# Mamba-2 stage of a four-layer network: VectorE in program order, convolution steps deferred, the group norm applied after the output product

## Chip, cores and metric

The kernel runs on one core of a Trainium2 chip. The metric is the device time of one execution in microseconds (us), as the median of three runs. A profile is one further execution under the hardware profiler.

## The reference

Four layers act on x of shape 2 x 1024 x 256 (float32), each as x = x + attention(LN x), then x = x + ffn(LN x):

- layer 0: causal attention with 16 heads and rotary positions; SwiGLU
- layer 1: grouped attention (16 query heads, 4 key heads) with two gates; SwiGLU
- layer 2: a Mamba-2 block in the place of attention; a ternary-weight feed-forward
- layer 3: a simple attention of rank 32; a mixture of 16 experts, the two best per token

The Mamba-2 block, to which the change belongs, computes (cut from the reference; H = 32 heads of 64, G = 8 groups, state S = 32):

```python
zxbcdt = (hidden_states @ W_in + b_in) * mup_vector
z, xBC, dt = ...                      # 2048, 2048 + 2*256, 32 columns
xBC = silu(causal_conv4(xBC) + conv_b)
x, B, C = ...                         # 2048, 256, 256 columns
dt = softplus(dt + dt_bias);  a = exp(dt * -exp(A_log))
state[t] = a[t] * state[t-1] + dt[t] * x[t] (outer) B[t]
y = state . C + D_param * x
y = y * silu(z)
y = y * rsqrt(mean over each group's 256 channels of y*y + eps) * norm_w
return y @ W_out + b_out
```

Since the group norm scales each token and group by one number, it may be applied before the product with W_out, or to the product's eight parts, one for each group, behind it.

## The kernel before

**Layout.** x stays in SBUF as 16 token tiles of 128 x 256, `xs[i]`. Before each stage `norm` (L93) writes the normalised x and its transpose `xnT`. One function, `tile_blocks_kernel`, holds all stages one after the other, and names its engines at its start (L46): V is VectorE, S ScalarE, G GpSimd (POOL in the profile), PE TensorE. Its helpers `norm`, `add_to_x` (L128), `evacuate` (L140, a copy from PSUM that ScalarE and VectorE take in turn), `softmax` (L150) and `ffn` (L157) use these names. Where nothing else is said, a scheduler decides each engine's order; `tc.keep_in_program_order(...)` fixes an instruction's place, in the order of the program, among those of its engine that are so marked, and `tc.high_priority()` asks for an early place.

**Mamba stage.** The 2048 tokens are 8 blocks of 256 (4 per batch). All TensorE and ScalarE work of the stage is kept in program order (helpers `pe`, `pe_t`, `act`, whose lines L702, L705 and L708 show in the profile); VectorE and POOL are scheduled. A block's x, B and C live channel by token: `quads[blk, q]` for q = 0 to 3 (groups q and q + 4, 128 x 4 x 256) and `bcs[blk]`. Per block:

- `steps2`: dt and dA from the product `dp`, a chain of small VectorE instructions (first `u`, L743).
- `project(blk, f)`, ten per block: product `xp_ps` in a PSUM bank of tag A (two banks, also for `gate` and the norm's `rg`); ScalarE writes xp and the fourth tap's part; six VectorE instructions (L809) add the other three taps of the convolution. `silu` follows.
- `prepare(blk, t, hs)`, four per block (two halves of 128 tokens, two pairs of quads): per group, POOL makes `dm` (L834), PE `lp`, ScalarE the decay `ml`. `from_start` makes `cd` from `rp`; `to_end` makes `de` from `ep` and `bt` (L886) from `bp`; `times_dt` transposes x (`xtp`) and VectorE makes `xd` (L850); `masked` makes `cp`, and VectorE `cm` (L897) and, shared with POOL, the masked `ml` (L900).
- `scan(blk, t, hs)`: `yp` gets xd times ml and the old state times cd. Then, for each quad, POOL makes dx = D x (L968, a tile with one buffer), and VectorE adds it to `yp` (L971). `sp` feeds the new state.
- `gate(blk, f)`, eight per block, one block behind: product `zp`; ScalarE's Silu, POOL's product with y (L1003), ScalarE's Square, in series. `squares` sums the squares of each group on PE into the bank Q (`qp`).
- The norm: `scales` takes the root (ScalarE) and the reciprocal of a 128 x 256 tile (L1020). `scaled(blk, q)` spreads the eight rows over the partitions by PE with the constant selT (`rg`, two products of 128 x 256 per quad) and VectorE multiplies y (L1028, 128 x 1024).
- `output(blk, t)`: 16 products `op` into one PSUM bank of tag Q, and `add_to_x` (L129).

The order is written out by hand. For each block four quarters i = 0 to 3 go by; in each, `prepare` works for the next quarter's scan, calls `scan` through `now()`, and at four places calls `fill()`, which takes a share of a list `work`: gates and squares of the block before (i = 0, 1), the projections of the next block (2, 2, 3, 3 in the four quarters), the norm (i = 2) and the output product (i = 3). What is left of the list comes at the quarter's end.

**Behind the Mamba stage** come the ternary feed-forward (`ffn`) and layer 3. There, routing finds the place of each token's two copies, and 32 indirect transfers (L1269) scatter the normalised tokens to `sent` in 47 slots of 128 rows. `attention(0)`, batch 0's attention, stands behind the scatter in the program. The expert loop then does for each slot s: load weights and rows, transpose the rows (`xgp`), VectorE copy `xgT` (L1332), 16 products `hp`, Silu `eh` (L1338), products `eo`, VectorE copy `ey` (L1343), store to `done` by POOL's queue. `attention(1)` follows, with a mask add, maximum, exponential, transposes, products and an add to x for each of eight query tiles; and at the end, for each of the 16 tiles of x, two indirect gathers `back` (L1351, eight buffers) that VectorE adds to x (L1356), and the store.

The code below has the lines of the profile.

Of the kernel before, what the change touches and what calls it, by code (L numbers as in the profile page):

```python
# [23 lines left out]
ALU = mybir.AluOpType  # L24
# [19 lines left out]
def kernel(ctx: ExitStack, tc: tile.TileContext, a: dict, out: bass.AP):  # L44
# [623 lines left out]
    selT = kept("selT", [P, 8, P])  # L668
    load(selT, a["selT"])
# [11 lines left out]
    with work_pool("l2") as pool, tc.tile_pool(  # L681
# [27 lines left out]

        def small(tag, blk, shape=(P, 2, 32), bufs=1):  # L710
            return pool.tile(list(shape), F32, tag=tag, name=f"{tag}_{blk}", bufs=bufs)
# [18 lines left out]
        def steps2(blk):  # L730
# [11 lines left out]
            with tc.high_priority():  # L742
                V.tensor_tensor(u, dp, heads(0), ALU.add)  # L743
# [29 lines left out]
        def project(blk, f):  # L773
# [32 lines left out]
            for n in range(2):  # L806
                for k in range(3):
                    c = 4 * (f + n) + k
                    V.scalar_tensor_tensor(  # L809
                        dst[:, n], xp[:, n, k : k + 256], cw[:, c : c + 1], dst[:, n],  # L810
                        op0=ALU.mult, op1=ALU.add,
                    )

        def silu(t_):
            tf = t_.rearrange("p f t -> p (f t)")
            act(tf, tf, AF.Silu)
# [4 lines left out]
        def prepare(blk, t, hs, fill, now):  # L821
# [22 lines left out]
            def times_dt(q):  # L844
# [4 lines left out]
                with tc.high_priority():  # L849
                    V.tensor_tensor(  # L850
                        xd.rearrange("p (a j) c -> p a j c", a=2),
                        tp.rearrange("p (a f) (h c) -> p a (f h) c", a=2, h=2),
                        by_quad(dt[:, t, :], q).unsqueeze(3).to_broadcast([P, 2, 4, 64]), ALU.mult,
                    )
# [20 lines left out]
            def to_end():  # L875
# [9 lines left out]
                with tc.high_priority():  # L885
                    V.tensor_copy(bt, bp)  # L886
                c["de"], c["bt"] = de, bt

            def masked(q):
# [6 lines left out]
                with tc.high_priority():  # L896
                    V.tensor_tensor(cm, cp, le.unsqueeze(1).to_broadcast([P, 2, P]), ALU.mult)  # L897
# [27 lines left out]
        def scan(blk, t, hs):  # L925
# [39 lines left out]
            for n, q in enumerate(qs):  # L965
                y = quads[blk, q][:, :, ct].rearrange("p (a f) t -> p a f t", a=2)
                dx = pool.tile([P, 2, 2, P], F32, tag="dx", name=f"dx{nm}_{q}", bufs=1)
                G.tensor_tensor(  # L968
                    dx, y, by_quad(Dp, q).unsqueeze(3).to_broadcast([P, 2, 2, P]), ALU.mult
                )  # L970
                V.tensor_tensor(y, yps[n], dx, ALU.add)  # L971
# [19 lines left out]
        def gate(blk, f):  # L991
# [31 lines left out]
        def scaled(blk, q):  # L1023
            rp = bank("A", [P, 2, 256], f"rg{blk}_{q}")
            for a in range(2):
                pe(rp[:, a], selT[:, q + 4 * a, :], gates[blk], True, True)
            y = quads[blk, q].rearrange("p (a f) t -> p a f t", a=2)
            V.tensor_tensor(y, y, rp.unsqueeze(2).to_broadcast([P, 2, 2, 256]), ALU.mult)  # L1028
# [20 lines left out]
        for blk in range(N2 + 1):  # L1049
            for i in range(4):  # L1050
# [424 lines left out]
```

## Time and profile before

| | |
|---|---|
| median of three runs | 3618.98 us (3617.89 to 3619.17) |
| the profiled execution | 3631.11 us, its span 3629.4 us |
| granted TensorE clock, mean | 0.930 |
| busy: PE, DVE, ACT, POOL | 3170.7, 1798.1, 1182.3, 1072.7 us |

By stretches of the program (the table of stretches; us):

| stretch | length | PE busy | DVE busy | clock |
|---|---|---|---|---|
| layer 0 (0 to 760) | 760 | 689.3 | 405.2 | 0.96 |
| layer 1 (to 2013) | 1253 | 1146.9 | 634.5 | 0.96 |
| Mamba (to 3072) | 1059 | 882.9 | 596.1 | 0.89 |
| ternary feed-forward (to 3215) | 143 | 135.1 | 38.7 | 0.98 |
| norm, routing, scatter, attention(0) (to 3362) | 147 | 76.5 | 52.1 | 0.68 |
| expert loop (to 3557) | 195 | 187.2 | 37.4 | 0.99 |
| attention(1), gather, store (to 3629.4) | 72 | 52.9 | 34.0 | 0.83 |

How the profile is read: DVE is VectorE, ACT ScalarE, PEld TensorE's weight loads, SP the queue that issues most DMAs. A group line gives the source line, the engine, the operation, what it writes and reads (names without numbers), shapes and count; then busy time and the mean duration in ns; then the engine's idle time just before such instructions and who ended it. A granted clock under 1 says that TensorE was throttled in part of the stretch. The line of an instruction that goes through a helper is the helper's.

### The profile page before, as it was taken

Reading aid. Unit: us, or ns where it says so; the run is one execution under the profiler, and the core shown is the slowest. Engines: PE = TensorE matmul, PEld = TensorE weight load, DVE = VectorE, ACT = ScalarE, POOL = GpSimd, SP = SyncE. Lnnn points to the kernel's source line nnn. Section 1 sums busy time; section 2 is a strip of 40 time slices with the busy share of each in tenths; the row PEclk is TensorE's granted clock in tenths of the full one; section 3 lists DMA queues with packets and bytes.
Section 4 is the critical chain, followed back from the end, with each engine's and each line's share of the span. In section 5 each row is a group of like instructions: output and inputs, shape, how many; then the busy total and the mean of one; then the engine's idle time right before and its main releaser. Section 6 shows DMA issues by size and latency. Waiting matters only on the chain.

```text
span 3629.4 us, 43224 instructions
## 1 busy us (share of the span) xinstructions
PE 3170.7 (87%) x16608; PEld 2062.8 (57%) x16608; DVE 1798.1 (50%) x3500; ACT 1182.3 (33%) x2089; POOL 1072.7 (30%) x1215
## 2 busy tenths in 40 slices
PE   7999999898998998988999788888788788984997
PEld 5666665544544544544555556666566566552885
DVE  5666553255465455565413775556546643241124
ACT  1133333332322322322312554644644542111111
POOL 2011101032233232232200565554555551013113
PEclk9999999799999999999999888989899899977998
DMA  4000100300000000000001000000000000003892
GB/s 135 7 19 13 48 1 1 127 1 1 1 0 1 1 1 0 1 12 30 1 21 35 1 1 1 1 1 1 1 1 1 1 17 14 1 4 110 287 319 79
DMA packets 80733, 117.24 MB, mean 32 GB/s; under 512 B 7664, under 2 KB 60848, under 8 KB 78992
## 3 DMA queue, kind: packets, MB, share of 16 engines
q1 hardware_dynamic: 66864, 91.67, 7.7%
q0 software_dynamic: 5328, 14.56, 1.2%
q10 hardware_dynamic: 8336, 8.26, 0.7%
q8 instruction: 131, 2.15, 0.2%
q14 instruction: 74, 0.61, 0.1%
HBM read 91.65 MB, written 22.81 MB: 32 GB/s over the span
## 4 chain that ended last, share of the span: by engine, by line
PE 61%; DVE 19%; ACT 8%; POOL 5%; issue 5%; DMA 1%; ACTq 0%; POOLq 0%; DVEq 0%; another core or an unknown queue 0%
PE op L126 7%; PE sc L126 6%; PE m L245 5%; DVE xx L809 4%; PE sc L245 4%; PE tp L631 3%; PE op L702 3%; PE d L126 3%; PE g L126 3%; PE u L126 3%; PE eo L126 2%; PE hp L126 2%; PE mx L245 2%; PE lp L702 2%; PE acc L245 2%
## 5 line engine op out<-in xcount | busy, mean ns | idle before, releaser
L622 POOL TENSOR_SCALAR pr<-pr,r,gate 128x128 f32<-128x128 f32 (+7 forms) x256 | 211.0, 826 | 535.6 <-DVE r L621 473.7
L154 ACT ACTIVATE pr<-sc,nmax 128x128 f32<-128x128 f32 (+7 forms) x272 | 201.3, 741 | 477.1 <-DVE nmax L153 411.3
L126 PE MATMUL sc<-kT,qT 128*128 128x512 f32 (+3 forms) x768 | 316.5, 515 | 41.9 <-POOL qT L578 29.0
L126 PE MATMUL op<-pT,v 128*128 128x512 f32 x576 | 287.0, 617 | 19.9 <-DVE pT L146 13.2
L809 DVE SCALAR_TENSOR_TENSOR xx<-xp,w2r,xx 128x256 f32<-128x256 f32 x384 | 223.5, 634 | 44.0 <-ACT xx L708 40.6
L339 ACT ACTIVATE pT<-sc 128x1024 f32<-128x1024 f32 (+1 forms) x160 | 150.3, 939 | 270.8 <-PE sc L245 270.8
L631 PEld LDWEIGHTS tp<-cst,pr 128*128 128x128 f32 x1152 | 137.7, 142 | 131.6 <-POOL pr L622 69.1
L153 DVE TENSOR_REDUCE nmax<-sc 128x1 f32<-128x128 f32 (+7 forms) x272 | 203.1, 754 | 6.2
L631 PE MATMUL tp<-cst,pr 128*128 128x128 f32 x1152 | 183.1, 282 | 17.6 <-POOL pr L622 13.4
L126 PEld LDWEIGHTS sc<-kT,qT 128*128 128x128 f32 x768 | 134.6, 206 | 112.4 <-POOL qT L578 39.3
L126 PEld LDWEIGHTS op<-pT,v 128*128 128x128 f32 x576 | 105.0, 192 | 153.5 <-issue 62.7
L144 ACT COPY pT<-tp 128x512 f32<-128x512 f32 (+2 forms) x160 | 91.9, 575 | 295.2 <-PE tp L631 255.2
L245 PE MATMUL sc<-qk,qk 32*128 32x256 f32 (+1 forms) x1280 | 169.2, 382 | 8.9 <-ACT pT L339 8.3
L146 DVE COPY pT<-tp 128x512 f32<-128x512 f32 (+2 forms) x152 | 103.6, 682 | 142.1 <-PE tp L631 134.7
L702 PE MATMUL lp<-dm,cst 128*128 128x512 f32 x256 | 149.2, 705 | 22.5 <-DVE u L743 11.4
L342 POOL TENSOR_SCALAR_AFFINE_SELECT pT<-pT 128x512 f32<-128x512 f32 x64 | 40.8, 637 | 428.2 <-ACT pT L339 424.8
L834 POOL TENSOR_TENSOR dm<-cst,dA 128x512 f32<-128x512 f32 x128 | 142.9, 1124 | 64.5 <-PE lp L702 62.6
L245 PE MATMUL mx<-qk,qk 32*128 32x256 f32 (+1 forms) x1280 | 144.7, 387 | 10.8 <-DVE nm L314 3.0
L245 PEld LDWEIGHTS sc<-qk,qk 32*128 32x128 f32 x1280 | 105.0, 186 | 66.6 <-issue 31.2
L708 ACT ACT_TABLE_LOAD x110 | 141.1, 1283 | 2.0
L151 DVE TENSOR_TENSOR sc<-sc,cst 128x128 f32<-128x128 f32 x272 | 79.6, 296 | 125.4 <-PE sc L126 120.5
L702 PE MATMUL xp_ps<-xnT,w2x 128*128 128x256 f32 x512 | 132.1, 404 | 7.1 <-ACT xx L708 6.7
(294 smaller groups left out, 6322.8 us busy)
## 6 DMA issues: line engine op xcount, KB each, us to landing
we<-in_L_W SPq DMA_DIRECT2D x94, 512.0 KB, 5.5
sent<-none ACTq DMA_DIRECT2D x1, 6016.0 KB
xg<-sent SPq DMA_DIRECT2D x47, 128.0 KB, 5.4
done<-ey POOLq DMA_DIRECT2D x47, 128.0 KB
gu<-in_L_gu SPq DMA_DIRECT2D x4, 1024.0 KB
x<-in_x ACTq DMA_DIRECT2D x16, 128.0 KB, 5.3
dn<-in_L_dn SPq DMA_DIRECT2D x2, 1024.0 KB, 8.3
tabs<-in_L_rope SPq DMA_DIRECT2D x2, 1024.0 KB
```

Source lines behind the costliest of these rows:

```text
L126: PE.matmul(out_, lhsT=lhsT, rhs=rhs, start=first, stop=last)
L146: V.tensor_copy(dst, src)
L153: V.tensor_reduce(nmax, sc[:, :n], axis=AX.X, op=ALU.max, negate=True)
L154: S.activation(pr, sc[:, :n], AF.Exp, bias=nmax, accum_out=total)
L245: tc.keep_in_program_order(PE.matmul(out_, lhsT=lhsT, rhs=rhs, start=first, stop=last))
L339: S.activation(pT[:, :, :, :w], sc[:, :, :, :w], AF.Exp, scale=0.25)
L622: G.tensor_scalar(pr[:, :n], pr[:, :n], r, gate[:, i, 4 * g + j : 4 * g + j + 1], op0=ALU.mult, op1=ALU.mult,)
L631: PE.transpose(tp[:, j, :], prs[j][:, kb * P : (kb + 1) * P], ident)
L702: tc.keep_in_program_order(PE.matmul(out_, lhsT=lhsT, rhs=rhs, start=first, stop=last))
L708: tc.keep_in_program_order(S.activation(*args, **kw))
L809: V.scalar_tensor_tensor(dst[:, n], xp[:, n, k : k + 256], cw[:, c : c + 1], dst[:, n], op0=ALU.mult, op1=ALU.add,)
L834: G.tensor_tensor(dm, le.unsqueeze(1).to_broadcast([P, 4, P]), dAc[:, 4 * g : 4 * g + 4].unsqueeze(2).to_broadcast([P, 4, P]), ALU.mult,)
```

## The change

The change touches six things:

1. An object `Ordered` stands for VectorE and marks each of its instructions to be kept in program order; V is set to it. The two `tc.high_priority()` blocks around `xd` and `cm`, and those around `u` and `bt`, go.
2. The six convolution instructions of a `project` are put on a list and issued by `convolve()`, which the next `fill()`, the next `silu` or the end of a quarter calls.
3. D x is no longer made by POOL: 32 VectorE instructions per block (128 x 128) compute y times D plus `yp` from PSUM.
4. The norm is applied behind the output product: the eight rows of sums are copied (`qs`), transposed by PE to tokens by groups (`qt`), root and reciprocal work on 128 x 16; `output` makes one product per group, in banks of tag A, and VectorE adds each, times its token's scale, to x. `scaled`, selT and its load go.
5. The Square of a gate is issued behind the next gate.
6. The work list: outputs of the first token half fall in quarter 2 and of the second in quarter 3, gates and projections alternate, and the silus move (quads 2 and 3 into the next block's first quarter).

The diff, without the four places where only a `tc.high_priority()` goes and without the constant selT on the host:

```diff
@@ before L665, after L665 @@
     nwD = rest2[:, 428 : 460]
     nw, Dp = nwD[:, 0:16], nwD[:, 16:32]
-    selT = kept("selT", [P, 8, P])
-    load(selT, a["selT"])
 
@@ before L707, after L705 @@
         def act(*args, **kw):
             tc.keep_in_program_order(S.activation(*args, **kw))
 
+        class Ordered:
+
+
+            def __getattr__(self, op):
+                return lambda *args, **kw: tc.keep_in_program_order(getattr(nc.vector, op)(*args, **kw))
+
+        V = Ordered()
+        convs = []
+
+        def convolve():
+            while convs:
+                convs.pop(0)()
+
         def small(tag, blk, shape=(P, 2, 32), bufs=1):
             return pool.tile(list(shape), F32, tag=tag, name=f"{tag}_{blk}", bufs=bufs)
 
@@ before L803, after L813 @@
                     bias=tap3[:, 1, g : g + 1], scale=tap3[:, 0, g : g + 1],
                 )
             G.tensor_copy(hist[:, f : f + 2, :], xp[:, :, 256:259])
-            for n in range(2):
-                for k in range(3):
-                    c = 4 * (f + n) + k
-                    V.scalar_tensor_tensor(
-                        dst[:, n], xp[:, n, k : k + 256], cw[:, c : c + 1], dst[:, n],
-                        op0=ALU.mult, op1=ALU.add,
-                    )
+
+            def step(n, k):
+                c = 4 * (f + n) + k
+                V.scalar_tensor_tensor(
+                    dst[:, n], xp[:, n, k : k + 256], cw[:, c : c + 1], dst[:, n],
+                    op0=ALU.mult, op1=ALU.add,
+                )
+
+            convs.extend(lambda n=n, k=k: step(n, k) for n in range(2) for k in range(3))
 
         def silu(t_):
+            convolve()
             tf = t_.rearrange("p f t -> p (f t)")
             act(tf, tf, AF.Silu)
 
@@ before L963, after L973 @@
                                     a == 1 and jj >= 2,
                                 )
             for n, q in enumerate(qs):
-                y = quads[blk, q][:, :, ct].rearrange("p (a f) t -> p a f t", a=2)
-                dx = pool.tile([P, 2, 2, P], F32, tag="dx", name=f"dx{nm}_{q}", bufs=1)
-                G.tensor_tensor(
-                    dx, y, by_quad(Dp, q).unsqueeze(3).to_broadcast([P, 2, 2, P]), ALU.mult
-                )
-                V.tensor_tensor(y, yps[n], dx, ALU.add)
+                for a in range(2):
+                    for f in range(2):
+                        y, g = quads[blk, q][:, 2 * a + f, ct], 2 * q + 8 * a + f
+                        V.scalar_tensor_tensor(
+                            y, y, Dp[:, g : g + 1], yps[n][:, a, f], op0=ALU.mult, op1=ALU.add
+                        )
             if not last:
                 if hs == 0:
                     c["sp"] = bank("T", [P, 2, 256], f"sp{nm}", bufs=1)
@@ before L1001, after L1011 @@
                 g = f + n
                 act(zs[:, n], zp[:, n], AF.Silu, bias=bm[:, g : g + 1], scale=mup_f[:, g : g + 1])
             G.tensor_tensor(y, y, zs, ALU.mult)
+            gates[blk, f] = zs, y
+
+        def square(blk, f):
+            zs, y = gates[blk, f]
             act(zs, y, AF.Square)
-            gates[blk, f] = zs
 
         def squares(blk, f, n_th):
             if n_th == 0:
@@ before L1010, after L1023 @@
             g = f // 2
             for n in range(2):
                 pe(
-                    gates[blk], sel[:, 7 - g : 7 - g + P], gates[blk, f][:, n],
+                    gates[blk], sel[:, 7 - g : 7 - g + P], gates[blk, f][0][:, n],
                     n_th == 0 and n == 0, n_th == 7 and n == 1,
                 )
 
+        def sums(blk):
+
+            qs = pool.tile([8, 256], F32, tag="qs", name=f"qs_{blk}", bufs=1)
+            V.tensor_copy(qs, gates[blk][0:8, :])
+            gates[blk] = qs
+
         def scales(blk):
-            rs = pool.tile([P, 256], F32, tag="rs2", name=f"rs2_{blk}", bufs=1)
-            act(rs, gates[blk], AF.Sqrt, scale=1.0 / 256.0, bias=eps_t)
+            qt = bank("Q", [P, 2, 8], f"qt{blk}", bufs=1)
+            for t in range(2):
+                tc.keep_in_program_order(
+                    PE.transpose(qt[:, t, :], gates[blk][:, t * P : (t + 1) * P], ident[0:8, 0:8])
+                )
+            rs = pool.tile([P, 2, 8], F32, tag="rs2", name=f"rs2_{blk}")
+            act(rs, qt, AF.Sqrt, scale=1.0 / 256.0, bias=eps_t)
             V.reciprocal(rs, rs)
             gates[blk] = rs
 
-        def scaled(blk, q):
-            rp = bank("A", [P, 2, 256], f"rg{blk}_{q}")
-            for a in range(2):
-                pe(rp[:, a], selT[:, q + 4 * a, :], gates[blk], True, True)
-            y = quads[blk, q].rearrange("p (a f) t -> p a f t", a=2)
-            V.tensor_tensor(y, y, rp.unsqueeze(2).to_broadcast([P, 2, 2, 256]), ALU.mult)
-
-        def output(blk, t):
-            op = bank("Q", [P, D], f"op2_{blk}_{t}", bufs=1)
+        def output(blk, t, gs):
+
+            op = bank("A", [P, 2, D], f"op2_{blk}_{t}_{gs[0]}")
             ct = slice(t * P, (t + 1) * P)
-            fs = [f for q in range(4) for f in (2 * q, 2 * q + 1, 2 * q + 8, 2 * q + 9)]
-            for n, f in enumerate(fs):
-                pe(op, quads[blk, n // 4][:, n % 4, ct], w2o[f // 8][:, f % 8, :], n == 0, n == 15)
-            add_to_x(2 * blk + t, op)
+            for n, g in enumerate(gs):
+                for f in range(2):
+                    pe(
+                        op[:, n], quads[blk, g % 4][:, 2 * (g // 4) + f, ct],
+                        w2o[g // 4][:, 2 * g % 8 + f, :], f == 0, f == 1,
+                    )
+            for n, g in enumerate(gs):
+                x = xs[2 * blk + t]
+                V.scalar_tensor_tensor(
+                    x, op[:, n], gates[blk][:, t, g : g + 1], x, op0=ALU.mult, op1=ALU.add
+                )
 
         V.memset(hist, 0.0)
         V.memset(state, 0.0)
@@ before L1051, after L1076 @@
                 t, hs = i // 2, i % 2
                 work = []
                 nxt, prv = blk + 1, blk - 1
-                if prv >= 0:
-                    if i < 2:
-                        four = xorder[4 * i : 4 * i + 4]
-                        for n, f in enumerate(four):
-                            work.append(lambda f=f: gate(prv, f))
-                            at_ = 4 * i + n
-                            if at_ >= 2:
-                                work.append(lambda n=at_ - 2: squares(prv, xorder[n], n))
-                        if i == 1:
-                            gated = [lambda n=n: squares(prv, xorder[n], n) for n in (6, 7)]
-                            gated.append(lambda: scales(prv))
+                old = prv >= 0
+
+                def outputs(t):
+                    return [lambda t=t, q=q: output(prv, t, (q, q + 4)) for q in range(4)]
+
+                if i == 0 and 0 < blk < N2:
+                    work += [lambda: silu(quads[blk, 2]), lambda: silu(quads[blk, 3])]
+                new = []
                 if nxt < N2:
                     pairs = ([16, 18], xorder[0:2], xorder[2:5], xorder[5:8])[i]
-                    for f in pairs:
-                        work.append(lambda f=f: project(nxt, f))
-                        if i == 3 and prv >= 0 and f != pairs[2]:
-                            work.append(lambda t=(f != pairs[0]): output(prv, int(t)))
+                    new = [lambda f=f: project(nxt, f) for f in pairs]
+                other = []
+                if old and i < 2:
+                    for n in range(4 * i, 4 * i + 4):
+                        def gated(n=n):
+                            gate(prv, xorder[n])
+                            if n:
+                                square(prv, xorder[n - 1])
+
+                        other.append(gated)
+                        if n >= 2:
+                            other.append(lambda n=n: squares(prv, xorder[n - 2], n - 2))
+                if old and i == 2:
+                    other.append(lambda: (squares(prv, xorder[6], 6), square(prv, xorder[7])))
+                    other.append(lambda: (squares(prv, xorder[7], 7), sums(prv)))
+                    other.append(lambda: scales(prv))
+                    other += outputs(0)
+                if old and i == 3:
+                    other += outputs(1)
+                while new or other:
+                    if new:
+                        work.append(new.pop(0))
+                    for _ in range(-(-len(other) // (len(new) + 1))):
+                        work.append(other.pop(0))
+                if nxt < N2:
                     if i == 1:
-                        work.append(lambda: (steps2(nxt), silu(bcs[nxt])))
-                    if i == 1 and prv >= 0:
-                        work[-2:-2] = gated
+                        work.append(lambda: (silu(bcs[nxt]), steps2(nxt)))
                     if i == 2:
                         work.append(lambda: silu(quads[nxt, 0]))
-                        work.append(lambda: silu(quads[nxt, 1]))
                     if i == 3:
-                        work.append(lambda: silu(quads[nxt, 2]))
-                        work.append(lambda: silu(quads[nxt, 3]))
-                elif i == 1 and prv >= 0:
-                    work += gated
-                if prv >= 0:
-                    if i == 2:
-                        for q in range(4):
-                            work.append(lambda q=q: scaled(prv, q))
-                    if i == 3 and nxt >= N2:
-                        work.append(lambda: output(prv, 0))
-                        work.append(lambda: output(prv, 1))
+                        work.insert(1, lambda: silu(quads[nxt, 1]))
                 if blk < N2:
                     if i < 3:
                         after = (blk, (i + 1) // 2, (i + 1) % 2)
@@ before L1095, after L1125 @@
                     share = len(work) // 5 or 1
 
                     def fill():
+                        convolve()
                         for _ in range(share):
                             if work:
                                 work.pop(0)()
@@ before L1109, after L1140 @@
                     else:
                         fill()
                         now()
+                convolve()
                 for w in work:
                     w()
     tc.no_sync_barrier()
```

In the changed kernel's built order TensorE has 9235 instructions (9283 before), VectorE 3782 (3502), ScalarE 1830 (1836), POOL 1156 (1220) and SP 515 (516). Up to the Mamba stage the instructions are the same, but for the load of selT.

More of the change, by code (lines that the diff above doesn't have):

```diff
@@ L741, in steps2 @@
             u = small("u", blk)
-            with tc.high_priority():
-                V.tensor_tensor(u, dp, heads(0), ALU.add)
+            V.tensor_tensor(u, dp, heads(0), ALU.add)
             V.tensor_tensor(u, u, heads(1), ALU.mult)
@@ L848, in times_dt @@
                 xd = pool.tile([P, 8, 64], F32, tag="xd", name=f"xd{nm}_{q}", bufs=3)
[L849 to L853, printed above, removed]
-                    )
+                V.tensor_tensor(
+                    xd.rearrange("p (a j) c -> p a j c", a=2),
+                    tp.rearrange("p (a f) (h c) -> p a (f h) c", a=2, h=2),
+                    by_quad(dt[:, t, :], q).unsqueeze(3).to_broadcast([P, 2, 4, 64]), ALU.mult,
+                )
                 c["xd"][q] = xd
@@ L884, in to_end @@
                 bt = pool.tile([P, 2, P], F32, tag="bt", name=f"bt{nm}")
-                with tc.high_priority():
-                    V.tensor_copy(bt, bp)
+                V.tensor_copy(bt, bp)
                 c["de"], c["bt"] = de, bt
@@ L895, in masked @@
                 cm = pool.tile([P, 2, P], F32, tag="cm", name=f"cm{nm}_{q}")
-                with tc.high_priority():
-                    V.tensor_tensor(cm, cp, le.unsqueeze(1).to_broadcast([P, 2, P]), ALU.mult)
+                V.tensor_tensor(cm, cp, le.unsqueeze(1).to_broadcast([P, 2, P]), ALU.mult)
                 for a in range(2):
@@ L965, in scan @@
             for n, q in enumerate(qs):
-                y = quads[blk, q][:, :, ct].rearrange("p (a f) t -> p a f t", a=2)
-                dx = pool.tile([P, 2, 2, P], F32, tag="dx", name=f"dx{nm}_{q}", bufs=1)
-                G.tensor_tensor(
-                    dx, y, by_quad(Dp, q).unsqueeze(3).to_broadcast([P, 2, 2, P]), ALU.mult
-                )
-                V.tensor_tensor(y, yps[n], dx, ALU.add)
+                for a in range(2):
[4 more added lines that the diff above has]
+                        )
             if not last:
@@ L1030, in output @@
-        def output(blk, t):
-            op = bank("Q", [P, D], f"op2_{blk}_{t}", bufs=1)
-            ct = slice(t * P, (t + 1) * P)
-            fs = [f for q in range(4) for f in (2 * q, 2 * q + 1, 2 * q + 8, 2 * q + 9)]
-            for n, f in enumerate(fs):
-                pe(op, quads[blk, n // 4][:, n % 4, ct], w2o[f // 8][:, f % 8, :], n == 0, n == 15)
-            add_to_x(2 * blk + t, op)
+        def output(blk, t, gs):
+            op = bank("A", [P, 2, D], f"op2_{blk}_{t}_{gs[0]}")
+            ct = slice(t * P, (t + 1) * P)
+            for n, g in enumerate(gs):
[8 more added lines that the diff above has]
+                    x, op[:, n], gates[blk][:, t, g : g + 1], x, op0=ALU.mult, op1=ALU.add
+                )
@@ L1374, in _constants @@
     cst[:, C_SEL + 7] = 1.0
-    selT = np.zeros((P, 8, P), f)
-    selT[np.arange(8), np.arange(8), :] = 1.0
     pos = np.arange(T, dtype=f)
@@ L1394, in _constants @@
     steps = np.concatenate([np.arange(16) * 128, np.arange(NSLOT)]).astype(f)
-    return {"cst": cst, "selT": selT, "L0_rope": rope0, "L1_rope": rope1, "eidx": eidx, "steps": steps}
+    return {"cst": cst, "L0_rope": rope0, "L1_rope": rope1, "eidx": eidx, "steps": steps}
 def _laid_out(i):
```

## The prediction

> **What bounds the kernel now.** I read the table of stretches first, one window for each of the five steady Mamba blocks (from one block's first output product `yp` to the next one's). One of them, and the sum (columns: length; busy time of PE, PEld, DVE, ACT, POOL; granted clock; DMA):
>
> ```profile
> 2406.67:2536.40 129.73, 109.20 (x669) 81.97 (x668) 75.92 (x130) 68.51 (x108) 64.05 (x73) 0.89 0.00 1
> ...
> sum 661.85, PE 554.79 PEld 416.42 DVE 380.92 ACT 342.36 POOL 344.33; mean PE 110.96 PEld 83.28 DVE 76.18 ACT 68.47 POOL 68.87
> ```
>
> A block takes 661.85 / 5 = 132.4 us. TensorE is busy for 111.0 of them, but at a clock of 0.89: as the clock is half or full, 22% of the block (29 us) ran at half, which loses 14.6 us. TensorE's work at full clock is thus about 111.0 - 14.6 = 96.4; passes counted at their full-clock price (256 columns 0.215 us, 512 columns 0.43) give 96.7. The waits view puts some 170 us of idle TensorE on the stage's 8 blocks, 21.6 per block. 96.7 + 21.6 + 14.6 = 132.9: that is the block. **TensorE in a fixed order, its waits, and the clock they cost** bound the stage; VectorE, at 76, does not. TensorE's rows of the timeline show the waits (columns: start, duration, operation, in brackets the idle time before it and who ended it):
>
> ```profile
> 2422.61 1.97 PE L705 MATMUL xtp<-cst,xx 128*128 128x128 f32 x8 [5.14 <-ACT ml L708]
> ...
> 2488.19 1.66 PE L702 MATMUL cp<-bc 32*128 32x128 f32 x8 [3.96 <-DVE xd L850]
> 2489.78 3.78 PE L702 MATMUL rg<-rs,selT 128*128 128x256 f32 x8
> 2496.95 3.78 PE L702 MATMUL rg<-rs,selT 128*128 128x256 f32 x8 [3.38 <-DVE xx L1028]
> ```
>
> Each steady block has four idles of 2.8 us or more: before `xtp` (4.8 to 5.1), `ep` (2.8 to 3.7), `cp` (4.0 to 4.7) and the second half of `rg` (3.4 to 4.5). Four idles to 29 us at half clock is 7.3 us each, 3.6 us lost by each.
>
> **The change, Mamba.** The groups by line price what goes:
>
> ```profile
> L809 DVE SCALAR_TENSOR_TENSOR xx<-xp,w2r,xx 128x256 f32<-128x256 f32 x276 | 160.0, 632 | 40.4 <-ACT xx L708 38.6
> L702 PE MATMUL rg<-rs,selT 128*128 128x256 f32 x96 | 44.1, 639 | 25.4 <-DVE xx L1028 25.4
> L968 POOL TENSOR_TENSOR dx<-xx,w2r 128x512 f32<-128x512 f32 x46 | 50.8, 1104 | 53.5 <-DVE xx L971 53.5
> L971 DVE TENSOR_TENSOR xx<-yp,dx 128x512 f32<-128x512 f32 x46 | 31.7, 689 | 29.4 <-POOL dx L968 19.7 <-PE yp L702 9.7
> L1028 DVE TENSOR_TENSOR xx<-xx,rg 128x1024 f32<-128x1024 f32 x24 | 28.7, 1214 | 9.1 <-PE rg L702 9.1
> ```
>
> - TensorE per block: 16 `rg` passes go (at full clock 16 x 0.215 = 3.4), two small transposes `qt` come (0.3, from the 128x128 transposes): 96.7 to about 93.7.
> - VectorE per block: out 8 x 0.689 (adding `dx`), 4 x 1.214 (scaling), the 128x256 reciprocal (1.75) and two adds of 128x256 (0.85), together 13.0. In 32 D-x-plus-scan instructions of 128x128 from PSUM (nearest row L151, same shape, 0.296; I take 0.31: 9.9), 16 of 128x256 adding the scaled output to x (L129 0.42, L1356 0.48: 7.2), a copy and a small reciprocal (0.65), together 17.8. 76.2 becomes 81.
> - POOL loses 8 x 1.104, 69 to 60. Every ScalarE instruction stays, but the Square of a gate now stands behind the next gate's Silu, so ScalarE no longer stands still for POOL's product.
> - VectorE's order is now the program's, with convolutions in bursts of six (3.8 us) or twelve. What waits behind them is the cost. I walked the built order of one block quarter by quarter. TensorE's waits: the `qt` transposes want the copy `qs`, which stands behind eight D instructions and six convolutions, 4.5 to 5 us (4.75); the shared bank pair "A" is freed by output additions behind convolutions and masks, 1.7 and 2.5; `ep` behind `cd`, 2; `lp` behind the copy `bt`, 3; Square 0.8; what is left of today's `xtp` and `cp` waits, (36.8 + 34.3) / 8 = 8.9 a block now, of which I keep half, 4.5. Sum 19.3, hardly less than 21.6: **new waits take the old ones' place**. But of these only the first is as long as the four idles above. One or two such idles cost 3.6 to 7.2; I take 5. The bounds: none (0), or as many as now (14.6).
> - Period: 93.7 + 19.3 + 5 = 118.0, a gain of 14.4 on each of six steady blocks, 86. Bounds from the walk alone, 105 to 128.
> - The first block (87.5 us, no norm work in it) gains perhaps 5. The last scan's tail: gates there run ScalarE, POOL, ScalarE in series at 2.92 us each; without the inline Square about 1.7, 7 x 1.2 = 8.5; reciprocal (3048.0) to the last addition (3071.5) is 23.5, of which `rg` and scaling (6.4) go. Together about 15 to 20; I take 18.
> - Mamba in sum: -86 - 5 - 18 = **-109** (bounds -30 to -185).
>
> On the clock: idles of 2.8 to 5.1 us go with 29 us at half clock per block here, while the expert loop below, with gaps under 1 us, holds 1.00. [...]
>
> **The change, behind Mamba.** The name V belongs to the whole function and the Mamba stage sets it anew without putting it back. So every VectorE instruction of the ternary FFN, of layer 3's attention, routing, expert loop and gather is kept in program order as well; the built order confirms it. That is the dear part.
>
> - Expert loop. Table of stretches and timeline, before:
>
> ```profile
> 3440.00:3480.00 40.00, 38.32 (x253) 34.86 (x253) 7.65 (x20) 5.71 (x10) 4.92 (x10) 1.00 0.95 322
> ```
>
> ```profile
> 3423.16 0.60 PE L1330 MATMUL xgp<-cst,xg 128*128 128x128 f32 x4
> ...
> 3423.42 0.60 ACT L1338 ACTIVATE eh<-hp 128x512 f32<-128x512 f32 x1 [3.04 <-PE hp L126]
> 3423.58 0.76 DVE L1332 COPY xgT<-xgp 128x256 f32<-128x256 f32 x2 [0.69 <-PE xgp L1330]
> ...
> 3424.07 1.99 PE L126 MATMUL eo<-we,eh 128*128 128x256 f32 x8 [0.31 <-ACT eh L1338]
> ...
> 3426.10 0.42 DVE L1343 COPY ey<-eo 128x256 f32<-128x256 f32 x1 [1.77 <-PE eo L126]
> ```
>
> Now two `xgT` copies run ahead, so the next slot's `hp` fills the Silu of this one: 4.08 us a slot, TensorE 96% busy, the DMA 95%. In the new order `xgT` of slot s+1 stands behind `ey` of slot s, which needs `eo` of s: `hp` 1.95 (16 passes of 0.11 and the last one's end), Silu 0.60, `eo` 1.99, `ey` 0.42, `xgT` 0.38 in series, with 0.25 of hand-overs: 5.59. 46 x 1.51 = **+70**. Between: 0 if the DMA still set the pace at 4.08, +80 with longer hand-overs. The row speaks for the upper part: 322 GB/s is what 4.08 needs; at 5.59 the DMA has slack.
> - Attention of batch 1 and the gather. Before, the last `ey` is at 3557.1 and the end at 3629.4, 72.3 us, in which attention and the 32 back-additions interleave:
>
> ```profile
> 3560.00:3600.00 40.00, 30.16 (x89) 17.27 (x88) 21.42 (x56) 9.83 (x22) 26.83 (x27) 0.74 0.39 115
> ```
>
> After, each query tile's VectorE instructions (mask add, maximum, reciprocal, scaled output, transposed copy, add to x) end before the next tile's begin, and all back-additions come after the last tile. A tile in series, from this window's rows (third to fourth tile): scores 0.9, add 0.29, maximum 0.67, exponential 0.88, transposes 0.64, copy 0.4, product 1.45, output 0.48, transposes 0.6, copy 0.42, product 1.0, add 0.42 = 8.2; eight tiles 66, about 13 more for start and a clock that falls further. Then, with 8 buffers filled ahead, 24 gathers at 1.3, landing 3, addition 0.5 and store 3.5 = 38. 117 against 72.3: **+45** (30 to 60).
> - Attention of batch 0 becomes as serial (67 to 80 us), but lies beside the scatter, 32 transfers at 2.7 us from 3263 to 3359, 50 us of which TensorE is idle already: 0. If that cover were gone, some 30. Norm and ternary weights in source order: +2 to 3.
>
> Together **+118** (100 to 132 with the loop as argued).
>
> **Sum.** -109 + 118 = +9. The profiled execution took 3631.1 us (span 3629.4), 12 above the median of 3619.0; the sums are differences, so they go on the median: about **3630**.
>
> **Rivals.**
> 1. Mamba close to TensorE's work: the bursts fit into the slack (VectorE is busy for 81 of 118), waits fall to 8, one idle costs 3.6: period 105, -27 x 6 - 23 + 118 = -67, 3552. For it: all four long idles lose their present releaser. Against: in each quarter two `xd`, two `cm` and eight D results free TensorE, and all now stand in one queue with the convolutions. Chance 0.22.
> 2. Slower, by one mechanism: the bursts. Of ten a block some four catch TensorE waiting for `xd`, `cm` or a D instruction, each for half a burst, 1.9 (7.6 together), and the idles stay long enough for the half clock of today's kind. Period 126 to 128, -35 - 23 + 118 = +60, 3675. It decides from a period of about 117, where -15.5 x 6 - 23 cancels +117. Chance 0.22.
> 3. The order behind Mamba costs little, the DMA keeping the loop at 4.08 (nearly the case that the change does no more than it is named for): -109 + 48 = -61, 3558. Against it: the loop's serial chain above. Chance 0.06.
>
> **How the numbers follow.** Forecast 3630 (3595 to 3665), 0.50. About 0.2% (7 us, 3612 to 3626) can be told from no change. Within the forecast 0.11 faster, 0.12 the same, 0.27 slower; rivals 1 and 3 faster, rival 2 slower: 0.39, 0.12, 0.49. The range reaches into rivals 1 and 2 until some 0.2 lies outside: 3555 to 3690.
>
> **What would show it.** The period of the steady blocks (118; 105; 127) and their clock; an idle of 4 to 5 us before `qt`; `rg` gone; the loop's pitch 5.6; from the last `ey` to the end 117. It is wrong if the loop stays near 4.1, or if the period is outside 112 to 124.

## The result and the profile after

The changed kernel takes 3659.3 us (median of four runs, 3657.9 to 3661.9) against 3618.7: ratio 1.0113, 95% interval 1.0096 to 1.0131, so 35 to 47 us slower. Its profiled execution has a span of 3660.1 us at a mean clock of 0.93, 30.7 longer than the span before.

Where those 30.7 us come from can be read with a ruler: take the same marks in both timelines, and subtract.

| stretch, from mark to mark | before | after | change |
|---|---|---|---|
| start to the first `yp` of block 0 | 2054.1 | 2058.4 | +4.3 |
| block 0 | 87.5 | 94.4 | +6.9 |
| six steady blocks | 794.1 | 695.9 | -98.2 |
| block 7 and the last block's gates, norm, output | 135.8 | 111.7 | -24.1 |
| ternary feed-forward, norm, routing, to the first scatter | 191.6 | 192.1 | +0.5 |
| first scatter to first `ey` | 107.9 | 108.6 | +0.7 |
| first `ey` to last `ey` (expert loop) | 186.1 | 260.8 | +74.7 |
| last `ey` to the end | 72.3 | 138.2 | +65.9 |

So up to the end of the Mamba stage the kernel became 111 us shorter, and two stretches behind it, whose code the diff does not touch, 141 longer. (The profiled execution of before lay 12 us above its median, that of after 2.5; the remaining 10 of the 40.6 us show in no profile. On the chips of the later runs the kernel before had medians of 3626 to 3633. Runs are therefore compared below as ratios to the kernel before on the same chip; 0.001 is 3.6 us.)

The table of stretches for the steady blocks of the changed kernel:

```profile
2268.08:2384.37 116.29, 102.96 (x675) 76.43 (x674) 85.05 (x166) 66.69 (x107) 61.27 (x69) 0.94 0.00 1
...
sum 580.63, PE 510.60 PEld 380.05 DVE 422.65 ACT 333.20 POOL 299.94; mean PE 102.12 PEld 76.01 DVE 84.53 ACT 66.64 POOL 59.99
```

The period is 116.1. VectorE is at 84.5 of 116, not the limit; the clock rose from 0.89 to 0.94. In windows of 1 us it is 0.5 or 1.00, or a mean of the two at an edge, and the eight passes of `xtp`, 1.97 us at 0.5 in the kernel before, take 1.04 at 1.00. So about 14 us per block are at half clock in place of 29, which loses 7.2. TensorE's work at full clock is 102.1 - 7.2 = 94.9, its idle time 116.1 - 102.1 = 14.0.

Of the four long idles none is left (the one before `ep` has shrunk to 1.8 us), and one has come, in TensorE's and VectorE's rows of the timeline just ahead of `qt`:

```profile
2328.58 1.13 PE L700 MATMUL qp<-zs,cst 128*128 128x256 f32 x4
...
2329.88 2.15 DVE L712 SCALAR_TENSOR_TENSOR xx<-xx,w2r,yp 128x128 f32<-128x128 f32 x8
2331.94 2.96 DVE L712 SCALAR_TENSOR_TENSOR xx<-xp,w2r,xx 128x256 f32<-128x256 f32 x6
2334.81 0.41 DVE L712 COPY qs<-qp 8x256 f32<-8x256 f32 x1
2335.27 0.38 PE L1040 MATMUL qt<-cst,qs 8*128 8x8 f32 x2 [5.56 <-DVE qs L712]
```

The sums `qp` are ready at 2329.7. The copy `qs` needs 0.41 us, but stands in VectorE's order behind eight D instructions and six convolutions, and TensorE waits 5.56 us for it. This is how the cost of a queue looks: the releaser is a short instruction, and the rows ahead of it on its engine show what it queued for.

The groups by line answer to those of before: D instructions of 341 ns, output additions of 483, the convolution at 615 (632 before).

```profile
L712 DVE SCALAR_TENSOR_TENSOR xx<-xp,w2r,xx 128x256 f32<-128x256 f32 x276 | 165.5, 615 | 6.6
L712 DVE SCALAR_TENSOR_TENSOR xx<-xx,w2r,yp 128x128 f32<-128x128 f32 x184 | 49.4, 341 | 31.7 <-PE yp L700 31.7
L712 DVE SCALAR_TENSOR_TENSOR x<-op,rs,x 128x256 f32<-128x256 f32 x92 | 44.4, 483 | 74.2 <-PE op L700 72.0
```

All of VectorE's lines behind the Mamba stage also read L712, the line of `Ordered`: the trace itself says that the order reaches there. In the expert loop, a stretch and then one slot of the timeline:

```profile
3300.00:3340.00 40.00, 30.04 (x186) 24.60 (x184) 5.29 (x14) 4.18 (x7) 3.77 (x7) 1.00 0.73 233
```

```profile
3400.58 1.99 PE L126 MATMUL eo<-we,eh 128*128 128x256 f32 x8 [0.53 <-ACT eh L1370]
...
3402.61 0.42 DVE L712 COPY ey<-eo 128x256 f32<-128x256 f32 x1 [4.90 <-PE eo L126]
3402.95 0.41 DVE L712 COPY xgT<-xgp 128x256 f32<-128x256 f32 x1
...
3403.47 2.02 PE L126 MATMUL hp<-xgT,we 128*128 128x128 f32 x16 [0.90 <-PE eo L126]
3405.33 0.38 PE L1362 MATMUL xgp<-cst,xg 128*128 128x128 f32 x2
3405.59 0.60 ACT L1370 ACTIVATE eh<-hp 128x512 f32<-128x512 f32 x1 [5.06 <-PE hp L126]
```

One slot is now a ring: `hp`, Silu, `eo`, `ey`, `xgT`, `hp`. The next slot's rows were transposed long before; their copy `xgT` may only not pass `ey`. From 3403.47 to the next `hp` at 3409.13 it takes 5.66 us. The DMA share fell from 0.95 to 0.73: the transfers now wait for the loop (SP's queue for `xgp` and `eo`, 70.6 of the 100 us from 3300). The profile puts the 0.90 us before `hp` down to `eo`, which had ended; what ended last is the copy in between, a slip that the rows correct.

The end, in two stretches (attention of batch 1, then the gather):

```profile
3522.00:3618.00 96.00, 68.98 (x182) 39.88 (x180) 21.17 (x51) 13.67 (x29) 8.63 (x9) 0.68 0.04 13
3618.00:3660.00 42.00, 0.00 (x0) 0.00 (x0) 15.43 (x33) 0.00 (x0) 24.21 (x24) 0.52 0.44 125
```

Before, these two ran beside each other. Now POOL waits 83 us, and only then come the other 24 gathers, with TensorE idle:

```profile
3617.88 0.42 DVE L712 TENSOR_TENSOR x<-yp,x 128x256 f32<-128x256 f32 x1 [1.29 <-PE yp L126]
3618.22 3.75 DVE L712 SCALAR_TENSOR_TENSOR x<-back,p,x 128x256 f32<-128x256 f32 x8
3618.96 1.12 POOL L1383 DMA_INDIRECT back<-done,posi  x1 [83.28 <-DVE x L712]
```

The first eight gathers fill the eight buffers. The ninth needs one of them back, and the addition that empties it stands in VectorE's order behind the last tile's addition to x.

### The profile page after: what moved, and what is told of

It is laid out like the page before. It is cut to its first block, busy times and chain, and to the rows that moved or that the text cites. A ratio compares the mean times of both kernels' runs of the same rounds, so it can differ in the third digit from the quotient of the medians.

```text
span 3660.1 us, 43327 instructions
## 1 busy us (share of the span) xinstructions
PE 3160.8 (86%) x16496; PEld 2023.6 (55%) x16496; DVE 1861.2 (51%) x3780; ACT 1170.8 (32%) x2083; POOL 992.7 (27%) x1151
## 5 line engine op out<-in xcount | busy, mean ns | idle before, releaser
L712 DVE SCALAR_TENSOR_TENSOR xx<-xp,w2r,xx 128x256 f32<-128x256 f32 x384 | 228.9, 613 | 9.1
L153 DVE TENSOR_REDUCE nmax<-sc 128x1 f32<-128x128 f32 (+7 forms) x256 | 191.1, 754 | 6.1
L146 DVE COPY pT<-tp 128x512 f32<-128x512 f32 x144 | 99.1, 688 | 134.6 <-PE tp L631 134.6
L342 POOL TENSOR_SCALAR_AFFINE_SELECT pT<-pT 128x512 f32<-128x512 f32 x64 | 40.6, 634 | 430.8 <-ACT pT L339 427.4
L706 ACT ACTIVATE xp<-xp_ps,w2r 128x256 f32<-128x256 f32 x160 | 90.2, 564 | 150.7 <-PE xp_ps L700 97.4
L712 DVE COPY ey<-eo 128x256 f32<-128x256 f32 x47 | 19.9, 424 | 232.5 <-PE eo L126 232.5
```

Source lines behind the costliest of these rows:

```text
L146: V.tensor_copy(dst, src)
L153: V.tensor_reduce(nmax, sc[:, :n], axis=AX.X, op=ALU.max, negate=True)
L712: return lambda *args, **kw: tc.keep_in_program_order(getattr(nc.vector, op)(*args, **kw))
```

## The experiments

The main theory after the result: the Mamba stage gained what was forecast, and the order that leaks behind it costs 75 in the loop and 66 at the end. Its rival: the Mamba change itself, or what it leaves behind, costs the time. Each kernel below was executed four times, and the kernel before on the same chip. A ratio is known to about 0.0017, so a difference of two to about 0.0024, an estimated 9 us.

### Behind the Mamba stage

**e1_v_back**: the changed kernel, with one line behind the Mamba stage:

```diff
     tc.no_sync_barrier()
+    V = nc.vector
```

> The changed kernel, with the name V set back to the scheduled VectorE behind the Mamba stage; nothing else. Theory (the order that leaks behind the Mamba stage costs the loss, the Mamba stage itself gains): against the changed kernel the loop gives back 75 us (pitch 5.70 to 4.08) and the stretch from the last ey to the end 66 us (138 to 72), so 3659 - 141 = 3518; counted from the kernel before, 3619 - 111 = 3508 (the 111 us by which the place of the routing's last copy moved between the two profiles). Steady Mamba period stays 116. Rival (the loss lies in the Mamba change itself or in what it leaves for later stages, the order behind it being harmless because the DMA paces the loop): within 20 us of 3659.

Measured: 3518.5, ratio 0.9697 (0.9681 to 0.9714). That is the theory's count from the kernel before (3508, a ratio of 0.969); its 3518 (0.972) is met only in microseconds, on a chip where the kernel before takes 3626. Loop and steady period (2265.98 to 2846.72 for five blocks, 116.1) are as forecast; from the last `ey` to the end it takes 73.7. A stretch of the loop:

```profile
3300.00:3340.00 40.00, 38.45 (x256) 34.98 (x255) 8.03 (x20) 5.97 (x10) 4.88 (x9) 1.00 0.95 321
```

TensorE is at 96% and the DMA at 0.95 again.

**e2_loop_and_tail_free**: the same line, but behind `attention(0)` in the program.

> The changed kernel, with V set back only behind attention(0) in the program: the order still holds in the ternary feed-forward, the last norm, the routing and attention(0), not in the loop, attention(1) and the gather. Theory: within 5 us of e1_v_back, since attention(0) in series lies beside the scatter of some 97 us. Rival (attention(0) in series delays the loop): 20 to 30 us over e1_v_back.

Measured: 3519.7, ratio 0.9704 (0.9688 to 0.9720), as e1. The order in the feed-forward, norm, routing and attention(0) costs nothing that can be told: attention(0) in series ends at 3249.9 in the changed kernel, with the last scatter's issue (3248.9).

**e3_tail_free**: the same line, ahead of `attention(1)`.

> The changed kernel, with V set back only ahead of attention(1): the loop keeps the fixed order (pitch 5.7), the end is free (72 us from the last ey, or somewhat less, as attention(1) may start beside a loop that leaves engines idle). Theory, with the terms 75 and 66 read from the two profiles: 3659 - 66 = 3593, or down to 3575. Rival (the DMA paces the loop, and the 5.7 is due to it): a pitch of 5.7 in e2 as well.

Measured: 3594.0, ratio 0.9916 (0.9899 to 0.9932). The pitch is 5.67 with the fixed order (260.7 / 46) and 4.04 without (e2), so the DMA does not pace the loop at 5.67. The difference between e3 and e2, 0.0212, is 77 us for the loop; that between the changed kernel (1.0113, on the first chip) and e3, 0.0197, 71 for the end.

**e4_order_only**: the kernel before, with V set to an `Ordered` behind its Mamba stage.

> The kernel before with VectorE in program order from behind the Mamba stage on; the Mamba stage is as before. Theory: the price of the leak alone, 3619 + 141 to 151 = 3760 to 3770. Rival (the loss comes from the Mamba change): 3619 within 20 us.

Measured: 3766.7, ratio 1.0389 (1.0371 to 1.0406), 140 us slower on its chip. The leak alone, without anything of the Mamba change, has the price that the profiles gave. The rival has fallen.

### Within the Mamba stage

The base is e1. These four and the next four ran on other chips; the ratios are compared.

**m1_no_order**: V is never set to `Ordered`.

```diff
-        V = Ordered()
         convs = []
```

> e1_v_back (the changed kernel with V set back behind the Mamba stage, 3518 on the first chip, period 116.2) with V never fixed: the scheduler orders VectorE in the Mamba stage too, all other parts of the change stay. Theory (what gains is the removal of the four long idles: rg gone, the Square moved, D with the scan's output, the work list; the fixed order is only a means): 0 to +25 us against e1, period 116 to 120. Rival (the fixed order itself is the gain): +50 us or more, period over 124.

Measured: ratio 0.9570 (0.9554 to 0.9586), 46 us better than e1, where the theory had 0 to 25 worse and the rival 50 or more worse. Neither foresaw the sign. The fixed order is no means to the gain: of the 156 us that the other parts gain (0.0430), it costs 46. Period 111.3, block 0 83.0 (94.3 in e1). In block 0 of the changed kernel the sum of TensorE's waits for `xd` is 10.6 us, and here 4.0; ahead of the first of these `xd`, twelve convolutions (7.27 us) stood in the order. The wait before `qt` is still 3.95 us: the scheduled order too puts D instructions and convolutions ahead of `qs`.

**m2_conv_now**: in e1 the convolution is issued in `project`, not one share later.

```diff
-            convs.extend(lambda n=n, k=k: step(n, k) for n in range(2) for k in range(3))
+            for n in range(2):
+                for k in range(3):
+                    step(n, k)
```

> e1_v_back with the convolution steps issued at once inside project, not one share later; VectorE still in program order. Theory (VectorE in order must not stand before ScalarE's copy of a projection that has just been issued): each of ten projections blocks VectorE for the product and four ScalarE passes, 1.9 + 4 x 0.57 = about 4 us, of which part falls on TensorE through xd and cm: +30 to +70 us, period 122 to 128. Rival (VectorE has 30 us of slack in 116, so its waits do not show): under +10 us.

Measured: ratio 0.9678 (0.9662 to 0.9695), period 116.0: no difference from e1 that can be told, and the theory was wrong. VectorE does wait for ScalarE's part of `xx`, 88 us in the five steady blocks where the changed kernel has no such wait, but it has the time, with 78.3 of 116.0 us busy. With VectorE in program order, deferring the convolutions gains nothing; with its order free it was not tried.

**m3_dx_on_pool**: in e1, D x by POOL and its addition by VectorE, as in the kernel before (`dx`, L968, L971 there).

> e1_v_back with D x made by POOL again (8 x 1.10 us per block, one buffer) and added by VectorE (8 x 0.69). VectorE 84.5 to about 79.5 per block, POOL 60 to 69. Theory: qs stands behind the D instructions in the order; now it stands behind two pairs of POOL and VectorE steps in series, 2 x (1.1 + 0.7) = 3.6 in place of 8 x 0.34 = 2.7, so the wait for qs grows by about 1 us, and others likewise: +5 to +15 us. Rival (VectorE's 5 us of work is what counts): -20 to -30 us.

Measured: ratio 0.9728 (0.9712 to 0.9745), about 11 us worse than e1, as the theory had it, though hardly clear of noise by the ratios; the period, 118.9 for 116.1, speaks for it. The wait before `qt` grew from 5.6 to 7.2.

**m4_qs_on_act**: in e1 the 8 x 256 copy goes to ScalarE.

```diff
-            V.tensor_copy(qs, gates[blk][0:8, :])
+            act(qs, gates[blk][0:8, :], AF.Copy)
```

> e1_v_back with the copy qs of the eight rows of sums made by ScalarE in place of VectorE, so that it does not stand behind eight D instructions and six convolutions. Theory (the 5.6 us idle before qt is that queue, and it costs its own length and some 4 to 7 us at half clock's difference): the idle falls to 1 us or so, 4.6 + 2 to 4 per block on seven blocks, less what the next wait in line (the reciprocal on VectorE behind the same queue, which now holds the output's banks) takes back: -15 to -45 us. Rival (the wait only moves to rs and the bank A): within 8 us.

Measured: ratio 0.9571 (0.9555 to 0.9587), 46 us better than e1, just beyond the far end of the theory's range. TensorE's row:

```profile
2320.90 0.28 PE L1040 MATMUL qt<-cst,qs 8*128 8x8 f32 x2 [0.46 <-ACT qs L706]
```

The wait fell from 5.6 to 0.46, the period from 116.1 to 108.8, the clock rose to 0.97. An instruction of 0.4 us cost 7.3 us a block, because of the queue it stood in.

**n1_no_order_qs_act**: m1 and m4 together.

> m1_no_order (VectorE scheduled everywhere; ratio 0.957 to the kernel before) with qs copied by ScalarE, as in m4. Theory (two separate costs: the wait for qs, still 3.9 us a block in m1, and other waits of the fixed order, 11 us of them in the first block): they add, -4 us and some 1 to 3 of clock on 7 blocks, -25 to -50 us against m1, ratio 0.943 to 0.950. Rival (m1 and m4 gained by the same thing, the wait for qs and its clock): within 8 us of m1, ratio 0.955 to 0.959.

Measured: 3437.2, ratio 0.9470 (0.9454 to 0.9486), 36 us better than m1 and 82 better than e1, where m1 and m4 sum to 92: two separate costs, which nearly add. The table of stretches:

```profile
2244.07:2349.82 105.75, 97.53 (x675) 73.56 (x674) 81.54 (x165) 67.01 (x108) 61.59 (x69) 1.00 0.00 1
...
sum 526.16, PE 485.39 PEld 366.79 DVE 405.34 ACT 334.73 POOL 303.20; mean PE 97.08 PEld 73.36 DVE 81.07 ACT 66.95 POOL 60.64
```

Period 105.2, clock 1.00 in this block, and in the five steady blocks no idle of TensorE above 2.0 us. This version beats both kernels; it is 5.3% faster than the kernel before.

**n2_no_order_norm_first**: m1 with `scaled`, selT and the bank Q back, norm ahead of the output product, both halves' outputs in quarter 3; the rest of the change stays.

> m1_no_order with the norm applied ahead of the output product again (rg from selT by TensorE, reciprocal of 128 x 256, VectorE's four products of 128 x 1024, output in the bank Q); the rest of the change stays. Theory (the norm's place is the main part of the gain): rg work 3.4, its wait of 3.4 to 4.5 and the reciprocal's 1.75 in front of it, with the clock 10 to 14 us per block, +70 to +100 us against m1 with the tail, ratio 0.977 to 0.985. Rival (the gain is in the Square and the work list): under +30.

Measured: ratio 0.9702 (0.9685 to 0.9718), 48 us worse than m1: less than the theory, more than the rival. Period 116.6; TensorE's work rises, and the projection now waits 4.4 to 6.1 us per block for the bank A, which `rg` holds until VectorE has scaled.

**n3_no_order_square_inline**: m1 with the Square directly behind POOL's product.

```diff
             G.tensor_tensor(y, y, zs, ALU.mult)
+            act(zs, y, AF.Square)
             gates[blk, f] = zs, y
```

> m1_no_order with the Square of each gate issued in gate again, right behind POOL's product. Theory: ScalarE in order stands for POOL's product 1.3 us at each of eight gates, and behind it wait ml (then lp, xtp) and xp: +3 to +8 us per block, +25 to +60 us, ratio 0.964 to 0.973. Rival (ScalarE, busy for 67 of 111 us, has room): under +10.

Measured: ratio 0.9728 (0.9712 to 0.9744), 57 us worse than m1, as the theory had it. The waits of the Mamba stage:

```profile
ACT zs L706 <- POOL xx L1012: 128.8, 64, 6.2
```

ScalarE stands for POOL at each of the 64 gates; in m1 11 times and 23.2 us. Period 119.5. An engine busy for 67 of 119 us still sets the pace, since its order is fixed and `ml` and `xp` stand behind the Square.

**n4_no_order_dx_pool**: m1 with D x by POOL.

> m1_no_order with D x by POOL (8 x 1.10 us per block, one buffer) and its addition by VectorE again. Theory, from m3 (+11 to +15 with the fixed order, where qs stood behind the pair of steps): the wait for qs grows by about 1 us here too, 0 to +12 us, ratio 0.957 to 0.960. Rival (VectorE's 5 us less work counts, once its order is free): -10 to -30.

Measured: ratio 0.9573 (0.9557 to 0.9589), as m1. With VectorE's order free, D and the scan's output in one instruction are worth nothing that can be told; the wait before `qt` is 4.2 us here for 3.95 in m1, where m3 lengthened it by 1.6. That m3's 11 us were that wait fits, but was not shown by itself.

## Why the prediction was right, and where its terms were off

The time lies in the range, near its upper end, and on the likeliest side: the forecast's case came true, with its two opposing sums, -109 against -111 for the Mamba stage and +118 against +142 behind it. That the first pair agrees to 2 us is partly luck: the steady blocks gave 12 more than forecast and the tail 6 more, and the first block with its start took 16 instead. Of the 30 us by which the time lies above 3630, some 20 are the stretch of attention(1) and the gather, and 10 stand between profiles and medians.

- **What bounds the stage**: right. Work, waits and clock (94.9 + 14.0 + 7.2) add to the period by the way they are read; the test is that the work is near the 93.7 counted ahead, and that the experiments move the other two: n1, whose TensorE instructions are the same, has TensorE busy for 97 of 105 at a clock of 0.98 to 1.00.
- **Period**: 118.0 forecast, 116.1 measured, with smaller waits (14.0 for 19.3) and a dearer clock (7.2 for 5). "An idle of 4 to 5 us before `qt`" came at 5.6; m4 shows that it was worth 7.3 us a block with its clock. The waits for bank A (2.9 for 4.2) and for `cd` (2.5 for 2) came about as walked. Two terms of the walk did not come: `lp` behind `bt` (3) and half of the old waits at `xtp` and `cp` (4.5) are not among TensorE's waits of the steady blocks.
- **First block and tail**: +11 with its start, for -5. The block itself took 94.4 for 87.5, at a clock of 0.82 for 0.90. m1 parts the causes: without the order it takes 83.0, so -5 was right for the rest of the change, and the order added 11.4. The largest part of these 11.4 that is seen is TensorE's waits for `xd` behind bursts of convolutions, the mechanism of rival 2: 10.6 us with the order, 4.0 without (9.1 in the kernel before). The tail gave 24 for 18.
- **The loop**: +70 forecast, +75 measured; e3 against e2 shows it alone at 77. It is the ring of five steps; rival 3 has fallen.
- **Attention(1) and the gather: mis-sized**, +45 forecast and +66 measured, most of the error. The gather part was right (38 for 42). The chain of eight tiles was priced from a middle tile, 8.2 us each, with 13 for the start and the clock, 79 in all; it took 96. The additions to x lie 10.4, 11.8, 11.5, 12.9, 14.7, 11.6 and 13.4 us apart. The product of the last tile alone takes 5.5 us (16 passes of 0.34) where the middle tile's was counted at 1.45, and the clock in 3522 to 3618 is 0.68 (0.50 from 3607 to 3613, at that product). A chain whose links grow is not its middle link times the count, when the clock falls as well.
- **Attention(0)** hidden beside the scatter: right (e2). Norm and ternary weights: +2 to 3 forecast, under 1 measured.
- **The clock**: the forecast gave a price to long idles alone, 5 us, and 7.2 were lost. In windows of 1 us the granted clock of the block from 2268.1 is 0.5 from about 2306 to 2309, 2333.5 to 2340 and 2350.5 to 2353.5, some 13 us, and 1.00 elsewhere. Each of the three stretches lies at one idle of TensorE: 1.8 us (to 2305.1), 5.6 (to 2335.3) and 2.2 (to 2350.4). So the long idle goes with 6.8 us at half clock, and each short one with 3.4. In m4's first steady block, 109.6 us at a clock of 0.97, the 6.8 are gone with the long idle. By that clock an estimated 6.6 us are left, and the rows are slow behind two idles: four `lp` take 3.48 us behind the one of 1.81 (1.88 elsewhere in the block), sixteen `op` 5.41 behind the one of 2.63 (eight take 1.89). In the kernel before, the block from 2406.7 has stretches of 10, 3.4 and 13.6 us, at idles of 5.1 and 2.9 us and, the last, at two of 4.0 and 3.4, so that the 7.3 us for each idle were a mean of unlike prices. A short idle does not always cost: those of 1.7 to 2.0 us in n1, two in each block, go with clocks of 1.00, 0.98, 0.98, 1.00 and 1.00, an estimated 1.7 us per block at half. How long an idle must be is not shown: the one of 1.81 us before `ep` was followed by half clock in the changed kernel's block, and went with 1.00 in n1's first.
- **Not foreseen**: that the fixed order is itself a loss inside the stage too (m1), 46 of the 156 us that the change holds without it. The prediction priced the waits of the order, and not what the scheduler makes of the same work.

What the gain of m1 over the kernel before consists of: the norm's place 48, the Square 57, D 1 (each by its removal from m1); about 50 of the 156 are left, for the work list, for the deferred convolutions and the priorities that went, and for what the parts do together. That rest was not taken apart.

## What to carry to other kernels

Look up how far a name reaches: an engine handle that is wrapped for one stage and not put back orders every stage behind it, and a copy that may no longer pass another turns an overlapped loop into a ring. Look at each short instruction that another engine waits for, and count what is queued ahead of it on its own engine: moving one 0.4 us copy to another engine gave 46 us with VectorE's order fixed, and 36 with it free. And try the change without its order: of this change the order was the part that lost, in its own stage and outside.

## What was unexpected of the hardware

With TensorE's instructions of the changed kernel and no idle of it above 2.0 us, the granted clock stays at 0.98 to 1.00 (n1), in a stage where it had been 0.89. Short idles went with half clock too: with none above 2.7 us the clock is 0.97 (m4), and in the changed kernel's block from 2268.1 idles of 1.8 and 2.2 us were each followed by 3.4 us at 0.5, as much together as the 6.8 at the idle of 5.6 us between them.
